# One row moved from TensorE to ScalarE and GpSimd, and a planned four-layer kernel put in a new order

## The chip, the core and the metric

The kernel runs on one core of a Trainium2 chip. Its engines work side by side, each through its own queue of instructions in order: TensorE (PE, with weight loads shown as PEld) multiplies matrices into PSUM, VectorE (DVE), ScalarE (ACT) and GpSimd (POOL) work element by element, and SyncE (SP) issues the transfers. They wait for each other by semaphores. The metric is the device time of one execution in microseconds, as the median of several runs; less is better.

## The reference

The input x has 128 graphs of 64 nodes with 512 features, in float32, and adj holds one 64 x 64 matrix for each graph. Four layers follow each other; each normalizes x, applies a ReLU, and adds its own result to x:

```python
# layer 0: H = (adj != 0); hconv(x, W) = D^-1 H B^-1 H^T (x W^T) + b
h = relu(layernorm(x)); t = layer_norm(relu(hconv(h, W1, b1)), gamma, beta)   # 512 -> 1024
x = x + hconv(t, W2, b2) + h                                                  # 1024 -> 512
# layer 1: s = (h w) a; A = softmax-like(tanh(s_i + s_j)) * adj
h = relu(layernorm(x)); x = x + A @ h @ w
# layer 2: attention with queries, keys and values, weight = adj * exp(q k)
h = relu(layernorm(x)); x = x + normalize(adj * exp((h Wq)(h Wk)^T)) @ (h Wv + bv)
# layer 3: transition P from adj * exp(leaky_relu(..)); three hops
h = relu(layernorm(x)); x = x + relu(sum_k (P^k h) Wk[k] + bk[k])
```

In layer 0 the inner normalization has a scale gamma and an offset beta for each of its 1024 features. The kernel folds them into the second product: W2's rows are multiplied by gamma, and the row beta x W2 (512 numbers) is added as a bias. That row is what the change computes in another way.

## The kernel before

The 8192 rows of x are cut into 16 groups of four tiles of 128 rows (two graphs a tile). All groups pass through layers 0 and 1 first, their x is stored to a scratch in DRAM, and then all groups pass through layers 2 and 3. The large products use Strassen's scheme: two tiles and two halves of the features make a 2 x 2 block, and seven products stand in for eight (`strassen`, L664, its matmuls at L682; `chained` for layer 2, L921; `product` for layer 3, L1087, its matmuls at L1112). The combinations of weights that the scheme needs are made once, in `combine` (L385), by VectorE subtractions at L394 to L397, for W1, W2 and w.

The functions of the layers don't issue instructions. They record operations in a `Graph`: an engine, an estimated cost, what is read and written, and a priority. `Graph.run` (L83) then plans: it keeps a clock for each engine and takes the operation that can start first by the estimates, and among equals the one with the lowest priority value. That order is written out into each engine's queue, and nothing in it moves at run time. A priority is the sum of a running value (`step`, scaled by `STRETCH`, with the group's `PERIOD1` or `PERIOD2`) and a shift, which `part(name)` (L294) takes from the table `AT` (L282). Buffers come from pools of few slots (`Buf`); which slot an operation gets is part of the plan, too.

The estimates are written beside the operations. A transfer costs its size at 380 KB per us or 0.34 us of SP, and lands `lat` later (2.0 us, or `LAT` = 2.5 in layers 2 and 3). Where the plan expects TensorE to stand for over 1 us and a PSUM slot is free, `fill` (L1183) puts matmuls of a 128 x 128 matrix of ones, the fillers (L1187), into the gap:

```python
        for _ in range(int(gap * FILL / (0.224 if filled else 0.448))):
            nc.tensor.matmul(ps[:, :P], ones, ones, start=True, stop=True)
```

Each float32 matmul shows as two instructions, two passes, in the profile.

What the change touches: `setup_l0` (L432) makes the row beta x W2. It multiplies each of the eight chunks of W2 (128 rows, 512 columns) by a one-column matrix from beta on TensorE (L438), copies the sum out of PSUM on ScalarE (L440), scales W2 in place by gamma on ScalarE (L442), and spreads the row over all partitions with a matmul against ones (L443) and a copy (L444). The row is the bias of `emit_y` (L710 on GpSimd, L712 on VectorE).

At the start, layer 2's weight matrix is made as well: `setup_l2` loads Wq and Wk in four pairs of blocks (into the four slots of `tmp`), multiplies them (L468), and stores the result (L475). `load_group` (L340, L346) loads adj and x of a group, `load_w` (L312) the weights.

Layer 1's matrix of a group (tile `bd`, L864) needs a row of denominators from another partition layout: `across` (L714) writes it to DRAM (L720) and reads it back spread out (L724). `left_mul_T` (L583) multiplies it with the tiles. `transposed` (L588) turns a tile by a ScalarE copy (L592), a transposing transfer (L593) and a second copy (L594). Layer 2 makes its sums of transposed tiles at L907.

Layer 3's weights are factors of seven 256 x 256 combinations, made during layers 0 and 1 by `setup_w3`, stored in DRAM, and streamed in again for every group: 14 loads a group at L1104, 768 or 576 KB, into three slots `wf`.

Of the kernel before, what the change touches and what calls it, by code (L numbers as in the profile page):

```python
# [10 lines left out]
AF = mybir.ActivationFunctionType  # L11
# [8 lines left out]
KD = D // P  # L20
KH = DH // P
# [147 lines left out]
def tile_adj_preln_d4(  # L169
# [6 lines left out]
    nc = tc.nc  # L176
# [33 lines left out]
    def size(shape):  # L210
        n = 1
        for d in shape[1:]:
            n *= d
        return n

    for two in TWO:
        both = work.tile([P, max(sum(size(shape) * n for _, shape, n in tags) for tags in two)], F32,
                         name="_".join(tag for tags in two for tag, _, _ in tags))
        for tags in two:
            at = 0  # L220
            for tag, shape, n in tags:
                for i in range(n):
                    v = both[:, at:at + size(shape)]
                    at += size(shape)
                    if len(shape) == 3:
                        v = v.rearrange("p (a b) -> p a b", a=shape[1])
                    elif len(shape) == 4:
                        v = v.rearrange("p (a b c) -> p a b c", a=shape[1], b=shape[2])
# [6 lines left out]
    w2m, wm = Buf("w2m"), Buf("wm")  # L235

    def view(mem, at, k, n):
        return mem[:, at:at + k * n].rearrange("p (c o) -> p c o", c=k)
# [3 lines left out]
    w2_sb = view(slots["w2m"][0], 0, KH, D)  # L242
# [9 lines left out]
    def c_mm(n, count):  # L252
        return 2 * count * max(n * 2 / 2400 + 0.0025, 0.111)
# [3 lines left out]
    def c_v(n, from_psum=False):  # L257
        return n / 960 + 0.155 + 0.05 * from_psum

    def pe(cost, fn, r, w):  # L260
        return G.op("PE", cost, fn, r, w)
# [4 lines left out]
    def act(cost, fn, r, w):  # L266
        return G.op("ACT", cost, fn, r, w)

    def pool(cost, fn, r, w):
        return G.op("POOL", cost, fn, r, w)  # L270

    def dma(kb, fn, r, w, issue=0.34, lat=2.0):
        return G.op("SP", max(kb / 380.0, issue), fn, r, w, lat)

    def quad(b):
        return b.t.rearrange("p (c k) -> p c k", c=4)

    FILL, LAT = 0.75, 2.5


    STRETCH, PERIOD1, PERIOD2 = (1.9884, 2.1221, 50.9861, 3.7462), 79.959, 161.557
    AT = {  # L282
        "x0": -2165.99, "apart": 359.07, "w1": 560.57, "b1": -128.79, "w2": 2266.0, "w": 629.08, "c1": 83.74, "l0":
        -235.81, "c2": 158.31, "l1": 2264.36, "c": -2424.06, "g0": -2117.86, "g1": -2122.8, "g2": -1819.53, "g3":
        -591.79, "g": -1886.72, "bq": -99.87, "l3": -7.89, "wg": -1139.97, "wp": 573.47, "beg0": -142.55, "beg1":
        62.01, "end00": -13.21, "end01": -32.01, "end11": -18.15, "new2": -7.11, "new3": -54.85, "end2": -9.77,
        "end3": 676.8, "load1": 485.14, "load2": 547.59, "m": -43.8, "h0": -30.46, "p0": -0.2, "z0": -80.08, "q0":
        9.15, "y0": -548.45, "h1": -32.41, "p1": -27.07, "z1": -26.16, "q1": -1.17, "y1": 3.58, "s": -28.4, "t0":
        14.62, "e0": 9.6, "t1": 5.71, "e1": -125.7, "hT": 311.43, "sh": 220.57, "lq": 604.06, "pt": 684.45, "v":
        70.12, "pv": 723.21, "s3": 659.55, "tt": 692.85, "a0": 741.32, "b0": -508.03, "a1": 777.21, "ws": 323.28,  # L290
        "load3": 129.62, "bk": 350.9,
    }

    def part(name):  # L294
        G.shift = AT[name]
# [4 lines left out]
    ones = const.tile([P, P], F32, name="ones")  # L300
# [13 lines left out]
    def wkeys(name, c0, c1):  # L314
        return [(name, c // 2) for c in range(c0 - c0 % 2, c1, 2)]
# [6 lines left out]
    def load_cols(name, src, k):  # L322
        sb = const.tile([P, k], F32, name=name)
        dma(8, lambda: nc.sync.dma_start(sb, src), [], [name])
        return sb
# [27 lines left out]
    def x_mid(g, t):  # L353
        return xmid[g, t], [("xmid", g, t)] + ([("xo", g - 1, t)] if g else [])

    part("x0")
    bq_c = load_cols("bq_c", bq, KD)
    load_group(0, x_in, AT["apart"])
    part("w1")
    load_w("w1", w1_sb, W1T)  # L360
# [3 lines left out]
    gb2 = const.tile([P, 2, KH], F32, name="gb2")  # L364
# [20 lines left out]
    def combine(name, w_, x_, kc, n, eng, olds=()):  # L385


        k2 = [w_[:, :kc, :], w_[:, kc:, :]]
        blk = lambda i, j: k2[i][:, :, j * n:(j + 1) * n]
        sub = {"DVE": nc.vector.tensor_sub, "POOL": nc.gpsimd.tensor_sub}[eng]  # L390
        cost = c_v(kc * n) * (1 if eng == "DVE" else 2)
        low, high = wkeys(name, 0, kc), wkeys(name, kc, 2 * kc)
        T1 = (name, "T1")
        G.op(eng, cost, lambda: sub(x_[:, 1], blk(1, 1), blk(0, 1)), [*low, *high], [(name, "x1"), *olds])  # L394
        G.op(eng, cost, lambda: sub(blk(0, 1), blk(0, 1), blk(0, 0)), [*low, (name, "x1")], [T1, (name, "given")])
        G.op(eng, cost, lambda: sub(x_[:, 0], blk(1, 1), blk(0, 1)), [*high, T1], [(name, "x0")])
        G.op(eng, cost, lambda: sub(x_[:, 2], blk(1, 0), x_[:, 0]), [*high, (name, "x0")], [(name, "x2")])  # L397
        B = {"11": (lambda c: blk(0, 0)[:, c, :], low), "21": (lambda c: blk(1, 0)[:, c, :], high),
             "22": (lambda c: blk(1, 1)[:, c, :], high), "T1": (lambda c: blk(0, 1)[:, c, :], [T1])}
        for i, key in enumerate(("T2", "T3", "T4")):  # L400
            B[key] = (lambda c, i=i: x_[:, i, c, :]), [(name, f"x{i}")]
        return B
# [28 lines left out]

    def setup_l0():  # L432

        p, row, pb = Buf("ps"), Buf("o"), Buf("ps")

        def mm():
            for c in range(KH):
                nc.tensor.matmul(p.t[0:1, :], gb2[:, 1, c:c + 1], w2_sb[:, c, :], start=(c == 0), stop=(c == KH - 1))  # L438
        pe(c_mm(512, KH), mm, ["gb2b", *wkeys(w2m, 0, KH)], [p])
        act(0.6, lambda: nc.scalar.copy(row.t[0:1, :], p.t[0:1, :]), [p], [row])  # L440
        for c in range(KH):
            act(0.72, lambda c=c: nc.scalar.activation(w2_sb[:, c, :], w2_sb[:, c, :], AF.Copy, scale=gb2[:, 0, c:c + 1]), ["gb2g"], [(w2m, c // 2)])  # L442
        pe(c_mm(512, 1), lambda: nc.tensor.matmul(pb.t, ones[0:1, :], row.t[0:1, :], start=True, stop=True), [row], [pb])  # L443
        act(0.6, lambda: nc.scalar.copy(bw2_b.t, pb.t), [pb], [bw2_b])  # L444

    def spread(col, dst, r, key):
# [63 lines left out]
    fac = [[dram.tile([P, n * 3 * P], F32, name=f"fac{f}_{n}") for n in (4, 3)] for f in range(7)]  # L510
    BLOCKS, FACS = ((1, 2, 6, 5), (7, 3, 4)), ((0, 2), (0, 1))
# [58 lines left out]
    def pre_ln(g, t, stats=None):  # L570

        xx, h = xt[g, t], Buf("h")
        nm, rs = stats or pre_stats(g, t)
        act(0.82, lambda: nc.scalar.activation(h.t, xx.t, AF.Relu, bias=nm.t, scale=rs.t), [xx, nm, rs], [h])  # L574
        return h
# [424 lines left out]
    def layer3(g):  # L1000
# [5 lines left out]
        for t in range(T):  # L1006
            h = pre_ln(g, t, stats[t])
# [6 lines left out]
        dn, rn, tr, tt = Buf("col"), Buf("col"), Buf("bd"), Buf("tt")  # L1014
# [72 lines left out]
        def product(f, F, chain, first):  # L1087
            (A, B), (ka, kb) = F
            if first:
                banks[chain] = [Buf("ps"), Buf("ps")]  # L1090
            X = Buf("xi")
            lo, hi = (lambda f_: f_()[:, :, 0, :]), (lambda f_: f_()[:, :, 1, :])
            x2, x3, x4 = ((lambda i=i: X.t[:, i]) for i in range(3))
            sub = nc.vector.tensor_sub
            dve(0.6, lambda: sub(x2(), lo(B), lo(A)), [*ka, *kb], [(X, 0)])
            dve(0.6, lambda: sub(x3(), hi(B), x2()), [*kb, (X, 0)], [(X, 1)])
            dve(0.6, lambda: sub(x4(), hi(A), x2()), [*ka, (X, 0)], [(X, 2)])
            lhs = {1: (lambda: lo(A), ka), 2: (lambda: hi(A), ka), 6: (x2, [(X, 0)]), 5: (lambda: lo(B), kb),
                   7: (x3, [(X, 1)]), 3: (x4, [(X, 2)]), 4: (lambda: hi(B), kb)}
            for n in range(2):  # L1100
                w_, p, q = Buf("wf"), banks[chain][n], len(BLOCKS[n])
                shift = G.shift
                part("ws")
                dma(q * 210, lambda n=n, w_=w_, q=q: nc.sync.dma_start(  # L1104
                    w_.t[:, :q].rearrange("p r k c -> p (r k c)"), fac[f - 1][n]), [("fac", f - 1, n, k, d) for k in range(3) for d in FACS[n]], [w_], lat=LAT)
                G.shift = shift
                for r, b in enumerate(BLOCKS[n]):
                    at, kl = lhs[b]

                    def mm(at=at, r=r, p=p, w_=w_, q=q):  # L1110
                        for k in range(3):
                            nc.tensor.matmul(inner(p, q)[:, r, :], at()[:, k, :], w_.t[:, r, k, :], start=first and r == 0 and k == 0,  # L1112
                                             stop=k == 2, skip_group_check=True)
                    pe(c_mm(P, 3), mm, [*kl, w_] if first and r == 0 else [*kl, w_, p], [p])
                    step(c_mm(P, 3))
# [53 lines left out]
        s3 = snapshot("X")  # L1169
# [9 lines left out]
    def step(us):  # L1179

        G.prio += us * stretch[0]
# [56 lines left out]
    for k in range(1, 3):  # L1238
        b = Buf("h")
# [71 lines left out]
```

## Time and profile before

| what | us |
|---|---|
| median of 3 runs | 2352.32 (2350.69 to 2354.56) |
| the profiled execution's own time | 2347.34 |
| its span, first to last instruction | 2345.6 |
| TensorE busy | 2301.3, 98% |
| VectorE busy | 1936.0, 83% |
| ScalarE busy | 1386.6, 59% |
| GpSimd busy | 1201.9, 51% |
| DMA: mean rate over the span | 151 GB/s |
| TensorE's granted clock, mean | 0.998 of full |

In the groups of instructions, a row gives the line, the engine, the operation, the tiles (result and sources), the count, then the busy time and the mean duration of one in ns, and behind the bar the idle time of the engine just before and what ended it. The time line has the start, the duration, the same names and count, and in brackets the idle time before. Tiles that share memory have a joint name: `w2m_wm_a_wf` holds W2 and w at first, and layer 3's operands and factors later. Fillers count as busy. Matmuls overlap, so the sum of their durations is larger than their busy time.

### The profile page before, as it was taken

What the parts mean: (1) busy time and instruction counts of PE and PEld (TensorE: products, weight loads), DVE (VectorE), ACT (ScalarE), POOL (GpSimd) and SP (SyncE); (2) the same over time, 40 slices, a digit from 0 to 9 for tenths busy, and PEclk for the clock granted to TensorE, in tenths of its full rate; (3) what the DMA queues carried; (4) which work ended last, traced back from release to release, by engine and by line L of the source; (5) the groups of instructions that cost most, each with busy time, mean ns of one, the idle gap of its engine ahead of it and who ended that gap; (6) DMA issues with size and microseconds to landing.
All of it is one profiled execution on the core that took longest, in us unless ns stands there. A gap on an engine that the chain in (4) does not pass through costs nothing.

```text
span 2345.6 us, 39929 instructions
## 1 busy us (share of the span) xinstructions
PE 2301.3 (98%) x14342; PEld 1876.8 (80%) x14342; DVE 1936.0 (83%) x4004; ACT 1386.6 (59%) x1986; POOL 1201.9 (51%) x1764
## 2 busy tenths in 40 slices
PE   9999999999999999999999999999999999999998
PEld 4676667776777767777688989999999999999998
DVE  7977887878878777787867888888889888888886
ACT  4656565665656756557556656655565656556642
POOL 5435566556565455553433554455455545455533
PEclk9999999999999999999999999999999999999999
DMA  7333342432333432223334888787888888798767
GB/s 265 85 76 74 82 103 72 106 83 72 95 84 99 89 77 69 70 73 66 89 89 134 235 230 224 211 223 207 242 231 220 230 213 215 211 252 227 214 184 234
DMA packets 403478, 355.13 MB, mean 151 GB/s; under 512 B 290896, under 2 KB 321872, under 8 KB 403280
## 3 DMA queue, kind: packets, MB, share of 16 engines
q1 hardware_dynamic: 403280, 352.58, 56.2%
q8 instruction: 113, 1.85, 0.3%
q14 instruction: 85, 0.70, 0.1%
HBM read 241.05 MB, written 44.33 MB: 122 GB/s over the span
## 4 chain that ended last, share of the span: by engine, by line
PE 75%; DMA 9%; DVE 9%; ACT 3%; POOL 2%; issue 2%; SPq 0%; DVEq 0%; POOLq 0%; ACTq 0%
PE ps L682 35%; PE ps L921 13%; PE ps L1112 13%; PE ps L583 5%; DMA w2m_wm_a_wf<-fac 4%; PE ps L1058 2%; PE ps L990 2%; DVE o L382 2%; PE ps L835 2%; DMA x<-xm 2%; PE ps L952 1%; DVE st L553 1%; DMA wa_q<-o 1%; PE ps L468 1%; DMA rw<-row 1%
## 5 line engine op out<-in xcount | busy, mean ns | idle before, releaser
L574 ACT ACTIVATE h<-x,nm,rs 128x512 f32<-128x512 f32 x384 | 307.0, 814 | 260.7 <-POOL nm L561 234.8
L1112 PE MATMUL ps<-w2m_wm_a_wf 128*128 128x128 f32 x2304 | 300.0, 276 | 3.8 <-DMA w2m_wm_a_wf<-fac 3.1
L1112 PEld LDWEIGHTS ps<-w2m_wm_a_wf 128*128 128x128 f32 x2304 | 279.4, 192 | 9.0 <-issue 2.0
L555 POOL TENSOR_SCALAR rs<-mv 128x1 f32<-128x1 f32 x320 | 102.5, 320 | 349.0 <-DVE mv L554 329.6
L682 PE MATMUL ps<-w2m_wm_a_wf,s_s_zz 128*128 128x256 f32 x1152 | 279.8, 380 | 0.7 <-DVE s_s_zz L674 0.5
L1112 PE MATMUL ps<-w2m_wm_a_wf,tmp_mB_xi 128*128 128x128 f32 x2016 | 262.3, 275 | 3.3 <-ACT h L574 1.7
L682 PEld LDWEIGHTS ps<-w2m_wm_a_wf,s_s_zz 128*128 128x128 f32 x1152 | 216.4, 190 | 48.1 <-issue 18.7
L1112 PEld LDWEIGHTS ps<-w2m_wm_a_wf,tmp_mB_xi 128*128 128x128 f32 x2016 | 244.9, 192 | 6.1 <-ACT h L574 3.0
L682 PE MATMUL ps<-w2m_wm_a_wf,rT_vu_tt 128*128 128x256 f32 x1024 | 237.2, 379 | 3.7 <-ACT rT_vu_tt L594 3.6
L682 PE MATMUL ps<-wa_mem,mT_sx 128*128 128x512 f32 x512 | 236.6, 593 | 0.2 <-ACT mT_sx L585 0.2
L682 PEld LDWEIGHTS ps<-w2m_wm_a_wf,rT_vu_tt 128*128 128x128 f32 x1024 | 193.2, 190 | 44.6 <-issue 12.4
L556 POOL TENSOR_TENSOR rs<-rs,mhalf 128x1 f32<-128x1 f32 x320 | 213.5, 667 | 26.6
L553 DVE BATCH_NORM_STATS2 st<-x 128x6 f32<-128x512 f32 x256 | 173.2, 680 | 17.0 <-DMA x<-xm 11.2
L682 PE MATMUL ps<-wa_mem,s_s_zz 128*128 128x512 f32 x384 | 180.0, 597 | 0.5 <-DVE z_hT L702 0.4
L682 PEld LDWEIGHTS ps<-wa_mem,mT_sx 128*128 128x128 f32 x512 | 96.9, 190 | 102.0 <-issue 96.6
L561 POOL TENSOR_SCALAR nm<-mv,rs 128x1 f32<-128x1 f32 x320 | 160.9, 504 | 30.4
L710 POOL TENSOR_TENSOR u<-u,row_sh 128x256 f32<-128x256 f32 x96 | 77.7, 822 | 170.7 <-DVE u L652 142.3
L592 ACT COPY o<-h 128x1024 uint16<-128x1024 uint16 x128 | 133.4, 1043 | 48.0 <-DVE h L1049 25.2
L583 PEld LDWEIGHTS ps<-bd,h 128*128 128x128 f32 x1024 | 128.7, 194 | 35.0 <-issue 17.1
L973 POOL TENSOR_TENSOR u<-u,wp_bv_bk 128x512 f32<-128x512 f32 x48 | 63.9, 1332 | 181.0 <-ACT u L625 180.8
L594 ACT COPY rT_vu_tt<-z_hT 128x1024 uint16<-128x1024 uint16 x128 | 147.8, 1160 | 10.8 <-DMA z_hT<-tmp_mB_xi 9.7
L822 ACT ACTIVATE z_hT<-z_hT,nm,rs 128x512 f32<-128x512 f32 x128 | 103.8, 813 | 73.3 <-POOL nm L561 73.3
(195 smaller groups left out, 5085.5 us busy)
## 6 DMA issues: line engine op xcount, KB each, us to landing
w2m_wm_a_wf<-fac SPq DMA_DIRECT2D x112, 768.0 KB, 5.8
w2m_wm_a_wf<-fac SPq DMA_DIRECT2D x112, 576.0 KB, 5.0
x<-xm SPq DMA_DIRECT2D x128, 256.0 KB, 3.9
x<-in_x_dram SPq DMA_DIRECT2D x64, 256.0 KB, 2.8
xm<-x SPq DMA_DIRECT2D x64, 256.0 KB, 2.3
out_dram<-x SPq DMA_DIRECT2D x64, 256.0 KB, 4.1
adj<-in_adj_dram SPq DMA_DIRECT2D x32, 256.0 KB, 4.2
fac<-wp_bv_bk SPq DMA_DIRECT2D x63, 128.0 KB, 2.0
```

The lines of the kernel that those rows point to most:

```text
L553: dve(0.69, lambda i=i: nc.vector.bn_stats(st.t[:, i, :], src(i)), [r[i]], [(st, i)])
L555: pool(0.32, lambda: nc.gpsimd.tensor_scalar_add(rs.t, mv.t[:, 1:2], EPS), [mv], [rs])
L556: pool(0.65, lambda: nc.gpsimd.tensor_tensor(rs.t, rs.t, mhalf, ALU.pow), [rs], [rs])
L561: pool(0.47, lambda: nc.gpsimd.tensor_scalar(nm.t, mv.t[:, 0:1], rs.t, -1.0, op0=ALU.mult, op1=ALU.mult), [mv, rs], [nm])
L574: act(0.82, lambda: nc.scalar.activation(h.t, xx.t, AF.Relu, bias=nm.t, scale=rs.t), [xx, nm, rs], [h])
L583: nc.tensor.matmul(quad(p)[:, c, :], h.t[:, c * P:(c + 1) * P], rhs(), start=True, stop=True)
L592: act(1.05, lambda: nc.scalar.copy(u16(planes.t).rearrange("p (q c) -> p q c", q=2), u16(src()).rearrange("p (c q) -> p q c", q=2)), ksrc, ...
L594: act(1.16, lambda: nc.scalar.copy(u16(dst()).rearrange("p c (k q) -> p c k q", q=2), u16(back()).rearrange("p (q c r) -> p c r q", q=2, c ...
L682: nc.tensor.matmul(p.t[:, :n], lhs()[:, c, :], rhs(c), start=first and c == 0, stop=c == kc - 1, skip_group_check=True)
L822: act(0.72, lambda half=half, rs=rs, nm=nm: nc.scalar.activation(half(), half(), AF.Identity, bias=nm.t, scale=rs.t), [(z, j), rs, nm], [( ...
L921: nc.tensor.matmul(pair(p.t)[:, o, :], a, b, start=first and o == 0 and c == 0, stop=c == 1, skip_group_check=True)
L1112: nc.tensor.matmul(inner(p, q)[:, r, :], at()[:, k, :], w_.t[:, r, k, :], start=first and r == 0 and k == 0, stop=k == 2, skip_group_check ...
```

## The change

`setup_l0` makes the row beta x W2 by eight ScalarE copies of W2's chunks, each scaled by its column of beta, and seven GpSimd additions of these copies (128 x 512). The matmul that spreads the row now sums over all 128 partitions as well. Three estimates change: the fillers' share of a gap (`FILL`, 0.75 to 0.5), the landing time of the streamed factors (0.8 us later), and the cost of VectorE's weight combinations (1.25 times). The bias bq is loaded in another place of the plan. All priorities are new: `STRETCH`, the periods, and every entry of `AT` (some left out here). As the plan follows from these, the order of the instructions changes on every engine, and the number of fillers as well.

```diff
-    FILL, LAT = 0.75, 2.5
+    FILL, LAT = 0.5, 2.5
...
-    STRETCH, PERIOD1, PERIOD2 = (1.9884, 2.1221, 50.9861, 3.7462), 79.959, 161.557
+    STRETCH, PERIOD1, PERIOD2 = (2.2519, 8.2241, 53.4307, 3.8206), 87.555, 166.876
     AT = {
-        "x0": -2165.99, "apart": 359.07, "w1": 560.57, "b1": -128.79, "w2": 2266.0, "w": 629.08, "c1": 83.74, "l0":
+        "x0": -2117.99, "apart": 200.73, "w1": 455.23, "b1": 843.47, "w2": 3279.78, "w": 178.43, "c1": -941.54,
...
+    part("bq")
+    bq_c = load_cols("bq_c", bq, KD)
     part("x0")
-    bq_c = load_cols("bq_c", bq, KD)
     load_group(0, x_in, AT["apart"])
...
-        cost = c_v(kc * n) * (1 if eng == "DVE" else 2)
+        cost = c_v(kc * n) * (1.25 if eng == "DVE" else 2)
...
-        p, row, pb = Buf("ps"), Buf("o"), Buf("ps")
-
-        def mm():
-            for c in range(KH):
-                nc.tensor.matmul(p.t[0:1, :], gb2[:, 1, c:c + 1], w2_sb[:, c, :], start=(c == 0), stop=(c == KH - 1))
-        pe(c_mm(512, KH), mm, ["gb2b", *wkeys(w2m, 0, KH)], [p])
-        act(0.6, lambda: nc.scalar.copy(row.t[0:1, :], p.t[0:1, :]), [p], [row])
+        row, pb = Buf("o"), Buf("ps")
+        for c in range(KH):
+            b = Buf("h") if c else row
+            act(0.65, lambda c=c, b=b: nc.scalar.activation(b.t, w2_sb[:, c, :], AF.Copy, scale=gb2[:, 1, c:c + 1]), ["gb2b", (w2m, c // 2)], [b])
+            if c:
+                pool(1.35, lambda b=b: nc.gpsimd.tensor_add(row.t, row.t, b.t), [b, row], [row])
         for c in range(KH):
             act(0.72, lambda c=c: nc.scalar.activation(w2_sb[:, c, :], w2_sb[:, c, :], AF.Copy, scale=gb2[:, 0, c:c + 1]), ["gb2g"], [(w2m, c // 2)])
-        pe(c_mm(512, 1), lambda: nc.tensor.matmul(pb.t, ones[0:1, :], row.t[0:1, :], start=True, stop=True), [row], [pb])
+        pe(c_mm(512, 1), lambda: nc.tensor.matmul(pb.t, ones, row.t, start=True, stop=True), [row], [pb])
...
-                    w_.t[:, :q].rearrange("p r k c -> p (r k c)"), fac[f - 1][n]), ..., [w_], lat=LAT)
+                    w_.t[:, :q].rearrange("p r k c -> p (r k c)"), fac[f - 1][n]), ..., [w_], lat=LAT + 0.8)
```

## The prediction

> **What bounds the kernel now.** I read the page's busy table first, then one line per stage, then TensorE's waits, and then the time line at the places that the change touches. Lines are those of the kernel before, unless said.
>
> ```profile
> PE 2301.3 (98%) x14342; PEld 1876.8 (80%) x14342; DVE 1936.0 (83%) x4004; ACT 1386.6 (59%) x1986; POOL 1201.9 (51%) x1764
> ...
> 0.00:180.00 180.00, 169.62 (x684) 110.07 (x685) 143.75 (x300) 98.99 (x139) 85.07 (x131) 0.98 0.48 141
> 180.00:1120.00 940.00, 936.53 (x4069) 672.79 (x4068) 755.68 (x1638) 577.54 (x806) 522.31 (x799) 1.00 0.35 82
> 1120.00:1330.00 210.00, 203.91 (x1263) 171.85 (x1262) 162.69 (x336) 127.01 (x180) 86.65 (x144) 1.00 0.49 132
> 1330.00:2260.00 930.00, 915.85 (x7625) 849.31 (x7624) 808.94 (x1611) 557.41 (x820) 476.98 (x652) 1.00 0.80 219
> 2260.00:2345.00 85.00, 75.38 (x707) 72.80 (x706) 64.95 (x123) 25.62 (x41) 30.91 (x42) 0.99 0.77 239
> ```
>
> TensorE bounds every stage (columns: window, its length, busy time of PE, weight loads, DVE, ACT, POOL; then granted clock, DMA share, GB/s). It idles 10.4 us in the first 180 us, 3.5 in the steady part of layers 0 and 1, 6.1 at the passage to layers 2 and 3, 14.1 in their steady part, 9.6 at the end: 44 us in all. That, the work taken off PE and the fillers are all that can be won.
>
> ```profile
> L1187 PE MATMUL ps<-ones 128*128 128x128 f32 x226 | 29.3, 287 | 1.0 <-DVE ones L301 1.0
> L438 PE MATMUL ps<-w2m_wm_a_wf,gb 128*1 128x512 f32 x16 | 7.0, 592 | 0.0
> ...
> PE ps L1112 <- DMA w2m_wm_a_wf<-fac: 9.6, 17, 1.3
> PE ps L583 <- DVE bd L864: 6.6, 7, 2.1
> PE ps L682 <- ACT rT_vu_tt L594: 3.6, 2, 2.6
> ```
>
> The fillers are 113 matmuls (two passes each), the one-column row eight. The three largest waits are for the streamed factors (17 times), for the matrix of layer 1, and for a transposed copy.
>
> ```profile
> 7.93 8.80 PE L468 MATMUL ps<-tmp_mB_xi 128*128 128x512 f32 x16 [2.95 <-DMA tmp_mB_xi<-in_Wk_dram]
> ...
> 43.60 7.03 PE L438 MATMUL ps<-w2m_wm_a_wf,gb 128*1 128x512 f32 x16
> ...
> 67.59 1.99 PE L682 MATMUL ps<-w2m_wm_a_wf,rT_vu_tt 128*128 128x256 f32 x8 [2.61 <-ACT rT_vu_tt L594]
> ...
> 151.44 5.40 PE L583 MATMUL ps<-bd,h 128*128 128x128 f32 x32 [2.08 <-DVE bd L864]
> ...
> 1246.89 5.52 PE L1187 MATMUL ps<-ones 128*128 128x128 f32 x48
> 1252.25 3.65 PE L921 MATMUL ps<-z_hT,wa_mem 128*128 128x256 f32 x16
> ```
>
> The row's matmuls have PE to themselves: nothing hides them. Some fillers end in a wait (67.59, 151.44), so they stood in time that was lost anyway; at 1246.89 the next matmul follows at once, so there the fillers may have held ready work.
>
> **Part by part.** I compare the two written orders. "Distance" is PE work between two instructions, a pass taken at 0.429 us for 512 columns, 0.216 for 256 and 0.111 for 128 (spacing of starts in the time line). By it PE has 2292.1 us of work before and 2272.3 after: 6.9 less for the row, 12.9 less for 58 fillers (113 become 55). Nothing else is taken off PE.
>
> (1) The row: 16 passes at 0.429 go, -6.9. The last matmul (L443) has 128 rows now instead of one, and the same 512 columns: 0.
>
> (2) What the row costs elsewhere. ACT gets eight copies; their nearest row is the scaling L442, 0.706 us each: 5.6 us. The scaling of a chunk, and DVE's combinations of W2, now wait for them; but the chunks land at 37 to 44 us, and ACT is busy 21.6 of the 40 us from 20 to 60. POOL gets seven additions of 128x512 like L799 (1.27 us; 1.47 in the first 180 us): 8.9 to 10.3 us. Five of them stand behind eight L799 and two groups of statistics, and the first L799 waited for its row until 45.1: 13 additions and 2.7 us of statistics end between 64 and 67. L443, behind which all of PE's queue stands, is reached after 36.3 us of PE work from the first product of layer 0, which I put at 25.0 in (3): at 61.3. So PE waits 3 to 5.5 us there. At the same place of the old order it waits 2.6 + 0.7 us (67.59, and the matmul after it), with 0.9 us of fillers ahead. One wait replaces the other: net 0, bounds -4 to +3.
> DVE meets the additions too: a combination (L395) took 2.27 us beside a POOL addition, and its neighbour 1.23 without: 1.04 each, 7.3 for seven. DVE is busy 37.8 of the 40 us from 20 to 60, so part of it reaches PE: +2, bounds 0 to +7.
> The Trainium skill ("SBUF — State Buffer", "Who interferes with whom") says that a VectorE instruction with two SBUF inputs and a GpSimd instruction that reads SBUF exclude each other for a whole instruction. By that rule the term would have 8.9 us of DVE time instead of 7.3, on the side against the change; the row says that less than a whole addition was lost. With the same part of it reaching PE the sum would be -12.6 by the rule and -13.0 by the row.
>
> (3) The start. Wq and Wk now lead SP's queue, ahead of adj and bq. The first 256 KB landed 3.2 us after its issue (1.18 to 4.40), the next 0.7 later, so L468 can start at 4.7 instead of 7.93. W1 goes behind the second weights, w and the second group: SP reaches it near 14.7 instead of 7.8, its halves land near 21.5 and 24.2 (18.4 before), and three combinations at the 5.7 us they took give T2 at 29.9. PE wants T2 at 30.2: just covered, and without that cover each us later is a us lost. So layer 0's first product moves from 28.5 to 25.0: -3.5, bounds -3.6 to 0.
>
> (4) The fillers. At the 13 places, the time from the first filler to the next real matmul sums to 38.6 us; without the first place (6.9, in (3)) and the one at 63.8 (3.8, in (2)) it is 27.9 us for 100 fillers, 0.28 each. The code sets fillers by the expected wait times FILL, so at 0.5 one filler stands for 1.5 times as much, 0.42. After has 46 beside the two places: 19.3 us. -8.6. Bounds: 0, if every filler dropped turns into idle; -12.0, if all 54 had held ready work.
>
> (5) The streamed factors. Their buffers are three; a load can start when the last matmul on its buffer is done. The distance from there to the first use is under 5.5 us (5.8 and 5.0 us from issue to landing) for 45 of 221 loads before, and for 18 after; those 18 are all near the end, as before. The steady part lost 7.3 us in 12 of the 17 waits: -5.5, bounds -7.3 to 0. The end keeps its 2.3 us.
>
> (6) Handoffs that are tighter. In the steady part of layers 0 and 1, the matrix of layer 1 (L864) is done 1.18 us ahead of its matmul (L583) by the order before, 0.20 after, in each of 11 groups. At 1.18, four groups waited 1.7 us in sum, since the two DMAs ahead of L864 vary (5.7 to 7.0 us from L862 to L864). +6, bounds 0 to 11. In layers 2 and 3, the last transposed copy (L594) stands 0.28 us ahead of L921 instead of 0.71 in 13 groups: +2.5, bounds 0 to 5.6. The sums L907, 0.63 instead of 2.28 ahead, waited already (2.8 us in 7): +1, bounds 0 to 8.
>
> (7) The clock: after the 2.1 us wait at 151.44, 32 passes took 5.40 us, and 3.73 at 71.24. Fewer fillers may add one such loss, or the shorter wait may drop it: 0, bounds -1.7 to +3.4.
>
> SP and POOL otherwise issue the same loads, stores and transposes in another sequence; between factor loads they stand much as before, so 0.
>
> Sum: -6.9 + 0 + 2 - 3.5 - 8.6 - 5.5 + 9.5 + 0 = -13.0. The profiled execution (span 2345.6, own time 2347.34) would come to 2334. It is 5 us under the median of the runs, 2352.32, and below all three; against that median I forecast 2339.
>
> **Rivals.**
> The fillers stood in real waits, and the start's gain is eaten by the late W1. Then (3) and (4) are 0 and -0.9 is left: 2351. For it: four of the places end in 1 us or more of idle. Against it: 47 of the fillers are followed at once by real work.
>
> Slower, by one mechanism: the transposed copy of layer 2. L594 waits for a DMA transpose, which SP issues in order behind factor loads that wait for PE (258.6 us of SP's waits). If the copy is 2 us late in each of 13 groups, PE stands 26 us: 2352.3 - 15.5 + 26 = 2363. It decides from 1.6 us a group on. For it: the distance was cut to 0.28. Against it: 0.71 gave one wait of 0.02 us in all of the steady part.
>
> The sums come later than I have them and L443 holds PE's queue: 10 us more than in (2) give 2349, 15 us 2354. For it: POOL's order has eight additions of b2 ahead of five sums. Against it: POOL was busy 25.9 of the 40 us from 20 to 60.
>
> **How the numbers follow.** A measurement here tells 0.2% (4.7 us) from no change. My forecast 0.58, with its own range 2322 to 2347; the fillers' rival 0.20, spread over faster, same and slower by 0.06, 0.09, 0.05; the copy 0.15, slower; the late sums 0.07, at 0.02, 0.02, 0.03. Faster 0.66, same 0.11, slower 0.23. All bounds together give -35 and +31; that all fall to one side is not to be expected, and 2320 to 2364 leaves out 2 in 10: the worse half of the copy's case and the late sums, and the better end of my own.
>
> **What would show it.** (1) no matmul of one column, eight ACT copies of 0.7 us. (2) L443 near 61 to 67 us, with a wait on POOL. (3) first L468 near 4.7, first product of layer 0 near 25. (4) fewer fillers and no longer idle after them. (5) waits for the factors at 2 to 4 us, at the end only. (6) waits of L583 for L864 in most groups, 0.3 to 1 us. (7) a clock at 1.0 beyond the first 20 us. I am wrong if the steady stages together idle over 30 us (17.6 now), or if the first product of layer 0 isn't earlier than 28.

## The result, and the profile after

The changed kernel takes 2364.26 us (median of 5 runs, 2358.70 to 2364.82), the kernel before 2352.72 on the same chip. The ratio is 1.0042, with a 95% interval of 1.0028 to 1.0057: slower by some 10 us, where I had forecast 13 us less. The profiled execution of the changed kernel is one of median time (span 2362.4); that of the kernel before lies 5 us under its median, so the two spans differ by 16.8.

The page's busy table, and the same stages as before (columns: window, its length, busy time of PE, weight loads, DVE, ACT, POOL; then granted clock, DMA share, GB/s):

```profile
PE 2289.1 (97%) x14210; PEld 1863.7 (79%) x14210; DVE 1938.5 (82%) x4004; ACT 1392.7 (59%) x1993; POOL 1212.5 (51%) x1771
```

```profile
0.00:180.00 180.00, 163.45 (x640) 105.92 (x641) 151.52 (x304) 104.22 (x147) 99.78 (x140) 0.98 0.48 141
180.00:1120.00 940.00, 934.83 (x4067) 672.49 (x4066) 774.63 (x1642) 581.68 (x804) 535.93 (x804) 1.00 0.34 82
1120.00:1330.00 210.00, 202.25 (x1214) 169.16 (x1213) 157.47 (x341) 131.36 (x187) 76.33 (x137) 0.98 0.51 133
1330.00:2260.00 930.00, 901.66 (x7493) 833.69 (x7492) 776.70 (x1572) 543.29 (x805) 461.79 (x643) 1.00 0.78 219
2260.00:2362.00 102.00, 86.87 (x802) 82.48 (x800) 78.14 (x149) 32.16 (x51) 38.65 (x49) 1.00 0.65 200
```

TensorE works 12.2 us less (2301.3 to 2289.1), and idles 29.3 us more: by stages 16.6, 5.2, 7.8, 28.3 and 15.1 us, against 10.4, 3.5, 6.1, 14.1 and 9.6. Half of it is new in the steady part of layers 2 and 3. The starts of the first sum L907 of a group say the same: between the fourth and the fifteenth group, 11 groups take 758.3 us before (1394.06 to 2152.37), 68.94 each, and 774.3 after (1392.25 to 2166.51), 70.39 each. At the fourth group the changed kernel is ahead by 1.8 us; over the 11 groups it loses 16.0, and behind them 2.7. This one execution shows less of a lead than the order has: at the third group it is 5.0 us ahead (1317.38 against 1322.35), while three of the later runs whose order is the same up to there (`copy_first`, `sums_first`, `both_first`: 1309.33, 1309.07, 1313.19) are ahead by 9.2 to 13.3. So the changed kernel comes to layers 2 and 3 with a lead, and loses more than that in them.

TensorE's waits over the whole run (total, times, longest):

```profile
PE ps L921 <- DVE row_sh L907: 22.0, 13, 2.3
PE ps L1037 <- DVE rT_vu_tt L1027: 8.4, 13, 2.6
PE ps L1112 <- DMA w2m_wm_a_wf<-fac: 8.3, 10, 3.1
PE ps L682 <- DVE u L654: 5.9, 4, 3.6
PE ps L583 <- DVE bd L864: 4.8, 7, 1.3
```

The sums L907 of layer 2 have taken the first place, with one wait in nearly every group (3.2 us in 8 waits before); the second, L1037 for L1027, stood at 0.2. I look at one steady group. VectorE's time line in it (start, duration, line, operation, tiles):

```profile
1526.96 1.67 DVE L383 SCALAR_TENSOR_TENSOR o<-h,c_b 128x512 f32<-128x512 f32 x1
...
1528.56 0.93 DVE L1049 TENSOR_TENSOR h<-h 128x256 f32<-128x256 f32 x1
1529.41 0.68 DVE L1131 TENSOR_TENSOR s_s_zz<-ps,s_s_zz 128x512 f32<-128x512 f32 x1
1530.01 0.89 DVE L1047 TENSOR_TENSOR h<-h 128x256 f32<-128x256 f32 x1
1530.82 1.21 DVE L383 SCALAR_TENSOR_TENSOR o<-h,c_b 128x512 f32<-128x512 f32 x1
...
1531.97 0.68 DVE L975 TENSOR_TENSOR rT_vu_tt<-ps,u 128x512 f32<-128x512 f32 x1
1532.57 0.68 DVE L907 TENSOR_TENSOR row_sh<-z_hT 128x512 f32<-128x512 f32 x1
```

ScalarE's and TensorE's in the same group:

```profile
1529.52 1.05 ACT L592 COPY o<-h 128x1024 uint16<-128x1024 uint16 x1 [1.65 <-DVE h L1049]
1530.47 1.16 ACT L594 COPY z_hT<-h 128x1024 uint16<-128x1024 uint16 x1
...
1533.30 1.99 PE L921 MATMUL ps<-wa_mem,row_sh 128*128 128x256 f32 x8 [2.06 <-DVE row_sh L907]
```

TensorE wants the first sum at 1531.24 and gets it at 1533.25. VectorE has no gap ahead of it: the dot products L383, which take 0.68 us alone, take 1.67 and 1.21, and L1049, L1047, L383 and L975 stand ahead of the sums. In all 12 steady groups these durations are the same within 0.02 us. In the kernel before only one dot product stands directly ahead of the sums, stretched as well (1462.02, 1.12 us); L1049 (1470.83), L1047 (1473.44) and L975 (1476.43) follow them, and the matmul that needs the sums starts without a wait. Its VectorE and TensorE at that place:

```profile
1462.02 1.12 DVE L382 SCALAR_TENSOR_TENSOR o<-h,c_b 128x512 f32<-128x512 f32 x1
1463.07 0.68 DVE L907 TENSOR_TENSOR row_sh<-z_hT 128x512 f32<-128x512 f32 x1
...
1464.53 3.72 PE L921 MATMUL ps<-row_sh,wa_mem 128*128 128x256 f32 x16
```

In the changed kernel the copy that the sums read (L594) is late too, by way of another engine: it stands on ScalarE behind L592, which waits for VectorE's L1049.

### The profile page after: what moved, and what is told of

The parts are those of the page before. It is cut to its first block, busy times and chain, and to the rows that moved or that the text cites. A ratio compares the mean times of both kernels' runs of the same rounds, so it can differ in the third digit from the quotient of the medians.

```text
span 2362.4 us, 39758 instructions
## 1 busy us (share of the span) xinstructions
PE 2289.1 (97%) x14210; PEld 1863.7 (79%) x14210; DVE 1938.5 (82%) x4004; ACT 1392.7 (59%) x1993; POOL 1212.5 (51%) x1771
## 3 DMA queue, kind: packets, MB, share of 16 engines
q8 instruction: 112, 1.84, 0.3%
## 4 chain that ended last, share of the span: by engine, by line
PE 67%; DVE 16%; DMA 9%; issue 3%; ACT 3%; POOL 2%; SPq 0%; DVEq 0%; ACTq 0%; POOLq 0%
PE ps L682 32%; PE ps L1112 13%; PE ps L921 11%; PE ps L583 4%; PE ps L1058 2%; DVE o L383 2%; DMA w2m_wm_a_wf<-fac 2%; PE ps L990 2%; PE ps L835 2%; DMA rw<-row 2%; DVE st L553 2%; DVE rT_vu_tt L1027 1%; DMA wa_q<-o 1%; DMA row<-col 1%; DVE tmp_mB_xi L1097 1%
## 5 line engine op out<-in xcount | busy, mean ns | idle before, releaser
L574 ACT ACTIVATE h<-x,nm,rs 128x512 f32<-128x512 f32 x384 | 302.2, 812 | 133.4 <-POOL nm L561 111.2
L682 PE MATMUL ps<-w2m_wm_a_wf,s_s_zz 128*128 128x256 f32 x1152 | 277.4, 380 | 0.2
L682 PEld LDWEIGHTS ps<-w2m_wm_a_wf,s_s_zz 128*128 128x128 f32 x1152 | 217.1, 190 | 44.1 <-issue 13.3
L682 PE MATMUL ps<-wa_mem,mT_sx 128*128 128x512 f32 x512 | 242.3, 597 | 7.7 <-DVE u L654 5.3
L682 PE MATMUL ps<-w2m_wm_a_wf,rT_vu_tt 128*128 128x256 f32 x1024 | 243.4, 382 | 0.9 <-DVE u L654 0.6
L682 PEld LDWEIGHTS ps<-w2m_wm_a_wf,rT_vu_tt 128*128 128x128 f32 x1024 | 193.8, 191 | 57.7 <-issue 30.7
L553 DVE BATCH_NORM_STATS2 st<-x 128x6 f32<-128x512 f32 x256 | 174.4, 685 | 17.5 <-DMA x<-xm 11.9
L682 PEld LDWEIGHTS ps<-wa_mem,mT_sx 128*128 128x128 f32 x512 | 96.3, 191 | 107.7 <-issue 88.0
L682 PE MATMUL ps<-wa_mem,s_s_zz 128*128 128x512 f32 x384 | 178.6, 593 | 2.4 <-DVE s_s_zz L674 2.4
L809 ACT ACTIVATE z_hT<-z_hT 128x512 f32<-128x512 f32 x128 | 80.1, 629 | 164.5 <-DVE z_hT L702 163.5
L561 POOL TENSOR_SCALAR nm<-mv,rs 128x1 f32<-128x1 f32 x320 | 151.0, 472 | 31.3
L592 ACT COPY o<-h 128x1024 uint16<-128x1024 uint16 x128 | 133.6, 1044 | 39.4 <-DVE h L1049 30.1
L594 ACT COPY rT_vu_tt<-z_hT 128x1024 uint16<-128x1024 uint16 x128 | 145.9, 1164 | 18.4 <-DMA z_hT<-tmp_mB_xi 17.9
L710 POOL TENSOR_TENSOR u<-u,row_sh 128x256 f32<-128x256 f32 x96 | 87.5, 926 | 123.6 <-DVE u L652 98.1
L921 PE MATMUL ps<-wa_mem,row_sh 128*128 128x256 f32 x512 | 121.0, 385 | 22.2 <-DVE row_sh L907 22.0
```

Of the source, the lines that this page charges most:

```text
L553: dve(0.69, lambda i=i: nc.vector.bn_stats(st.t[:, i, :], src(i)), [r[i]], [(st, i)])
L561: pool(0.47, lambda: nc.gpsimd.tensor_scalar(nm.t, mv.t[:, 0:1], rs.t, -1.0, op0=ALU.mult, op1=ALU.mult), [mv, rs], [nm])
L592: act(1.05, lambda: nc.scalar.copy(u16(planes.t).rearrange("p (q c) -> p q c", q=2), u16(src()).rearrange("p (c q) -> p q c", q=2)), ksrc, ...
L594: act(1.16, lambda: nc.scalar.copy(u16(dst()).rearrange("p c (k q) -> p c k q", q=2), u16(back()).rearrange("p (q c r) -> p c r q", q=2, c ...
L682: nc.tensor.matmul(p.t[:, :n], lhs()[:, c, :], rhs(c), start=first and c == 0, stop=c == kc - 1, skip_group_check=True)
L710: pool(0.75, lambda: nc.gpsimd.tensor_add(U.t[:, iv], U.t[:, iu], row()[:, cols]), [u, krow], [v])
```

## The experiments

All are edits of one of the two kernels. Ratios are to the kernel before, run on the same chip; the changed kernel's is 1.0042 [1.0028, 1.0057]. "Group" is the time of one of the 11 groups named above. In kernels with added lines the numbers of lines are larger by up to 12; the text names them by the lines of the changed kernel.

**The copy and the sums earlier in their queues.** A helper moves an instruction up past `hop` others of its engine, after the planning; all else keeps the changed kernel's order.

```diff
+        for x in [x for x in order if x[2].hop]:
+            i, n = order.index(x), x[2].hop
+            j = i
+            while n:
+                j -= 1
+                n -= order[j][2].eng == x[2].eng
+            order.insert(j, order.pop(i))
...
+            G.ops[-1].hop = 1 if t == T - 1 and 3 <= g < NG - 1 else 0      # copy_first: the last L594 of hT
...
+            G.ops[-1].hop = 2 if 3 <= g < NG - 1 else 0                     # sums_first: L907
```

> In 12 steady groups of layers 2 and 3 the last copy of hT (L594) goes one place up in ScalarE's queue, ahead of the split copy L592 that waits there 1.65 us for VectorE's L1049; all else keeps the changed kernel's order. Theory 'two queues' (PE's new wait of 19.9 us at L921 is made by VectorE's queue and by ScalarE's queue together): alone it brings nothing, 0 to -3 us, because the sums L907 still stand behind L383 and L975 on VectorE, which end at 1532.57 in the group that I looked at. Rival 'the copy alone' (the copy is what the sums wait for): the wait falls by about 1 us a group, -12. Rival 'not there' (the loss is not in this wait): 0.

> In the same 12 groups the four sums L907 go two places up in VectorE's queue, ahead of L383 and L975; the copy L594 stays behind L592. Theory 'two queues': the first sum can start when the copy ends (1531.63 instead of 1532.57 in that group), so about 0.9 us a group are won, -8 to -11. Rival 'VectorE's queue alone': the whole wait goes, -18 to -20. Rival 'not there', or 'the delay moves on' (L383, L975 and what follows them now come 2.8 us later and PE waits for those): 0 or slower.

> Both moves together. Theory 'two queues': the first sum ends at about 1531.5 where PE wants it at 1531.24, so 1.5 to 1.75 us in each of 12 groups are won: -18 to -21, the kernel near 2344 and below the kernel before by 6 to 9. The wait of L921 for L907 falls from 22 to under 5. Rival 'the delay moves on': the wait reappears at L990 (for L975) or L1058, and less than 8 us are won.

Measured: the copy alone 1.0038 [1.0026, 1.0051], the sums alone 1.0057 [1.0042, 1.0072], both 1.0045 [1.0029, 1.0060]; groups of 70.81, 70.87 and 70.80. Nothing is won, where the theory of two queues wanted nothing from the copy alone, but 8 to 11 us from the sums and 18 to 21 from both. TensorE's waits in the steady part, with the sums moved alone (its L929 is L921, its L630 ScalarE's copy of u, L623, and its L914 the sums):

```profile
PE ps L929 <- ACT u L630: 14.4, 12, 1.2
PE ps L929 <- DVE row_sh L914: 5.9, 7, 1.6
```

The wait for the sums fell from 19.9 to 5.9 us, and 14.4 us of waits for ScalarE have come in its place, once a group. The delay moves on, as the rival had it, but by way of ScalarE, which the rival didn't name. The link shows in ScalarE's queue: L592 waits for L383, though it needs nothing from it. Both write into slots of `o`, L383 the products that nobody reads. So a later L383 holds ScalarE's queue. From 1330 to 2250 us these waits sum to 6.0 us in the changed kernel, 18.4 with the copy moved, 40.2 with the sums moved and 48.5 with both. One of them, with the sums moved (its L599 is L592, its L390 L383):

```profile
1528.65 1.04 ACT L599 COPY o<-h 128x1024 uint16<-128x1024 uint16 x1 [3.35 <-DVE o L390]
```

**The additions thinned, on both kernels.** The edit leaves most of GpSimd's additions L1140 to L1143 and L973 out in the steady groups (each of the two places has its own K).

```diff
-            z = lambda a, b, s=1: Z.t[:, a:b:s]
+            z = lambda a, b, s=1: Z.t[:, a:b:s, :K]
+            K = 8 if 2 <= g < NG - 1 else P
...
+        K = 16 if 3 <= g < NG - 1 else D // 2
...
-                pool(1.42, lambda: nc.gpsimd.tensor_add(pair(U.t[:, iv]), pair(U.t[:, iu]), bias()), [u, bv_b], [v])
+                pool(1.42, lambda: nc.gpsimd.tensor_add(pair(U.t[:, iv])[:, :, :K], pair(U.t[:, iu])[:, :, :K], bias()[:, :, :K]), [u, bv_b], [v])
```

> The order of the changed kernel, but GpSimd's additions of the output (L1140 to L1143) and of layer 2's values (L973) handle an eighth or less of their columns in the steady groups, so most of this work is left out. Theory 'stretched by additions' (VectorE is late at L907 because L383, L1049 and L1047 take 1.67, 0.93 and 0.89 us beside GpSimd's additions instead of 0.68 and 0.5): VectorE reaches L907 1.5 to 2 us earlier, the wait shrinks from 19.9 to under 8, -10 to -16 us. Rival 'too much in the queue anyway': VectorE is as late as before, the wait stays above 15, and the time moves by less than 4.

> The kernel before, with the same of GpSimd's additions thinned as in the run 'thin' (most of L1140 to L1143 and L973 left out in the steady groups). There the changed kernel won some 33 us and its steady group of layers 2 and 3 went from 70.4 to 67.9 us; the group of the kernel before takes 68.8. Theory 'order times additions' (without the additions beside VectorE the two orders are equally good, TensorE bounds both): the group comes to 67.6 to 68.2, the time falls by 10 to 16 us. Rival 'the additions cost both the same': the group falls by 2.5 to 66.3, the time by 30 or more.

Measured: the changed kernel comes to 0.9905 [0.9884, 0.9926], 32 us less, where I had expected 10 to 16; the kernel before to 0.9968 [0.9952, 0.9983], 7.5 us less. The groups come to 67.87 and 68.48. In the steady part of the thinned changed kernel one wait for the sums is left, and the dot products have their short duration again (groups of instructions from 1330 to 2250 us, the dot products of the kernel before, where they are L382, of the changed kernel, and of the thinned changed one: count, busy time, mean ns of one; then TensorE's wait):

```profile
L382 DVE SCALAR_TENSOR_TENSOR o<-h,c_b 128x512 f32<-128x512 f32 x107 | 94.6, 902 | 0.9 <-DMA h<-o 0.9
```

```profile
L383 DVE SCALAR_TENSOR_TENSOR o<-h,c_b 128x512 f32<-128x512 f32 x104 | 94.5, 909 | 1.0 <-DMA wa_q<-o 0.9
```

```profile
L383 DVE SCALAR_TENSOR_TENSOR o<-h,c_b 128x512 f32<-128x512 f32 x109 | 74.8, 688 | 6.6 <-DMA wa_q<-o 5.7 <-DMA h<-o 0.4 <-ACT h L574 0.3
```

```profile
PE ps L921 <- DVE row_sh L907: 0.9, 1, 0.9
```

TensorE's waits for L1027, 5.8 us in the steady part of the changed kernel, are gone too, which the expectation had left out. So the order costs nothing by itself: without the additions the new one is the better by 0.6 us a group. The additions cost it 2.5 us a group and the old one 0.5 (7.5 us in all, where I had expected 10 to 16). The dot products are stretched alike in both, 902 and 909 ns on average; in the new order the stretch falls where TensorE waits for what comes next. The edit shortens GpSimd's own work as well, and doesn't separate that from the stretch: VectorE's waits for GpSimd's L1143 fell from 8.9 to 1.0 us. TensorE itself has no wait for GpSimd in its list.

**Undoing the link.** The dot products get a tile of their own for what nobody reads; the last kernel also moves the second half of L1027 ahead of two products (L960).

```diff
+    junk = const.tile([P, D], mybir.dt.bfloat16, name="junk")
...
-        dve(0.77, lambda: nc.vector.scalar_tensor_tensor(j.t, in0(), 1.0, in1(), op0=ALU.mult, op1=ALU.mult,
+        dve(0.77, lambda: nc.vector.scalar_tensor_tensor(junk, in0(), 1.0, in1(), op0=ALU.mult, op1=ALU.mult,
...
+            G.ops[-1].hop = 2 if i and 2 <= g < NG - 1 else 0               # all_first: L1027
```

> The changed kernel in its order; the dot products L383 write the products that nobody reads into a tile of their own (bf16) instead of a slot of o, which they share with ScalarE's split copies L592. So L592 no longer waits for a late L383 (0.5 us in the group that I looked at). Theory 'the queues are coupled through o': the copies come a little earlier, but the sums L907 still stand behind L383 and L975: 0 to -5. Rival 'o is the cause of the whole wait': -15 or more.

> As 'both_first' (the copy L594 one place up, the sums L907 two), with the tile of its own for the dot products. In 'both_first' the wait of 18 us at L921 for the sums became one of 14.2 us in 12 groups for ScalarE's copy of u, since L592 waited for the L383 that had been moved back, and ScalarE's queue with it. Theory 'the delay moved on through o': this wait falls under 4 us, the group from 70.7 to 69.4 to 69.8, the time by 10 to 14 against the changed kernel, to 0 to -4 against the kernel before. Rival 'VectorE has too much ahead of PE in any order of these few': another wait of 10 us or more takes its place, and the time stays.

> As 'both_junk', and the second half of L1027's transposes goes ahead of the two products L960 on VectorE, in groups 2 to 14, since TensorE waits 0.45 us for it in each group (5.4 to 6.8 us in all runs of the changed kernel). Theory: 3 to 5 us less than both_junk. Rival 'the delay moves on' to L990, which needs the products L960: 0.

Measured: the tile alone 1.0044 [1.0029, 1.0059]; with the copy and the sums moved 1.0007 [0.9997, 1.0016]; with L1027 as well 0.9988 [0.9978, 0.9998]. Groups of 70.48, 69.56 and 69.19. TensorE's largest waits in the steady part of the last (its L932 is L921, L632 is L623, L1001 is L990, L986 is L975):

```profile
PE ps L932 <- ACT u L632: 2.7, 9, 0.4
PE ps L1001 <- DVE rT_vu_tt L986: 2.7, 12, 0.2
```

That settles the chain. Neither the places in the queues nor the shared slots are enough alone, and together they give back 8 of the 10 us, where I had expected 10 to 14, and 13 with L1027; the last kernel is 0.12% faster than the kernel before (0.02 to 0.22%). That the new tile has another type (bf16) isn't what helps: with the tile alone the dot products still take 904 ns on average, and L592 waits for none of them. The delay has moved on a little even here, to L990 with 0.2 us a group, as the rival had it.

**The row.** Its copies and additions are left out, but for the first copy.

```diff
-            act(0.65, lambda c=c, b=b: nc.scalar.activation(
+            act(0.65, lambda c=c, b=b: c or nc.scalar.activation(
...
-                pool(1.35, lambda b=b: nc.gpsimd.tensor_add(row.t, row.t, b.t), [b, row], [row])
+                pool(1.35, lambda: None, [b, row], [row])
```

> The changed kernel in its own order, with seven of the eight copies L438 and all seven additions L440 left out, so the row is not the whole sum. Theory 'the additions slow VectorE at the start' (five of them run from 67.06 to 74.48 us, and beside them VectorE's L769 and L770 take 1.3 us each and TensorE waits 3.58 us for L654): the waits between 60 and 80 us fall by 3 to 5 us, and the time by 4 to 7. Rival 'VectorE is full there anyway': 0 to -2.

Measured: 1.0037 [1.0025, 1.0048], 1 us less than the changed kernel, which the intervals don't tell from nothing. The place is as expected, the total isn't. VectorE with the additions L440 (GpSimd's line first, then VectorE's), and without them:

```profile
67.06 7.42 POOL L440 TENSOR_TENSOR o<-o,h 128x512 f32<-128x512 f32 x5
...
67.57 2.69 DVE L769 TENSOR_SCALAR bd<-adj 64x256 f32<-64x256 f32 x2
70.28 1.32 DVE L770 TENSOR_SCALAR tmp_mB_xi<-adj 128x256 f32<-128x256 f32 x1
71.53 0.68 DVE L654 TENSOR_TENSOR u<-ps,u 128x512 f32<-128x512 f32 x1
```

```profile
67.71 0.58 DVE L769 TENSOR_SCALAR bd<-adj 64x256 f32<-64x256 f32 x2
68.30 0.29 DVE L770 TENSOR_SCALAR tmp_mB_xi<-adj 128x256 f32<-128x256 f32 x1
68.51 0.68 DVE L654 TENSOR_TENSOR u<-ps,u 128x512 f32<-128x512 f32 x1
```

L654 comes 3.0 us earlier, and TensorE idles 14.5 us in the first 180 instead of 16.6.

**The fillers**, in the changed kernel's order.

```diff
-    FILL, LAT = 0.5, 2.5
+    FILL, LAT = 0.75, 2.5
```

> The changed kernel with FILL at 0.75 again; the order is the same, 85 fillers instead of 55. Theory 'fillers stand in time that is lost' : 0 plus or minus 2 in sum, with the first 16 passes of L468 at 8.8 to 9.5 us instead of 10.06 (8.80 with 18 filler passes before them, 10.06 with 10), so -0.5 to -1.2 there. Rival, as my forecast had it: 0.28 us for each of 30 fillers, +8.

Measured: 1.0036 [1.0022, 1.0049], where the changed kernel has 1.0042. Thirty fillers more cost nothing, and save nothing that can be told. The 16 passes of L468 took 9.94 us, not the 8.8 to 9.5 that I had expected.

**The first transfers.** The pair of loads that the first pass of L468 needs goes to the front of SP's queue.

```diff
+            G.ops[-2].hop = G.ops[-1].hop = 0 if o else 3        # in setup_l2, the loads of Wq and Wk
```

> The changed kernel in its order, but the loads of Wq and Wk that the first pass of L468 needs go three places up in SP's queue and are now the first two (in the changed kernel they are the fourth and fifth transfers, and the first two feed the second pass). Theory 'wrong pair' (my forecast let L468 start when the first two transfers land, and they are the other pair): the first pass starts at 4.2 to 4.5 us instead of 6.76, the second waits for the other pair until 5.7 to 6.1; all 16 passes end 0.5 to 1.5 us earlier, and the total moves by less than 2, since layer 0 waits for VectorE later on. Rival 'the start counts in full': -2.4.

Measured: 1.0041 [1.0027, 1.0055]. TensorE's time line (its L476 is L468, its L789 L781):

```profile
4.32 8.82 PE L476 MATMUL ps<-tmp_mB_xi 128*128 128x512 f32 x16 [0.78 <-DMA tmp_mB_xi<-in_Wk_dram]
...
19.46 0.69 PE L789 MATMUL ps<-tmp_mB_xi,bd 128*64 128x65 f32 x16 [2.58 <-DVE tmp_mB_xi L783]
```

It was the wrong pair, as supposed. The passes start 2.4 us earlier and end 3.7 earlier (13.1 instead of 16.8), and the total doesn't notice: the next waits take more than half of it (layer 0's first product starts at 27.05 instead of 28.58), and the rest doesn't show in the total.

**VectorE's queue at the start**, on top of the last kernel.

```diff
+    for k, n in (269, 4), (276, 2), (278, 3):       # L674, L652, L654 of the first 75 us
+        G.ops[k].hop = n
```

> As 'all_first', and in the first 75 us three kinds of VectorE's work that TensorE waits for go ahead of work that nobody waits for soon: L654 ahead of the three products from adj (L769 twice, L770; they took 2.69 and 1.32 us beside the row's additions, and TensorE waited 3.58 us), L652 ahead of one L674 and one L485 (1.52), the first L674 ahead of four instructions (1.79). Theory 'the start's gain went into VectorE's queue': the three waits fall from 6.9 us to under 2, and 3 to 6 us are won against 'all_first' (0.9988 of the kernel before), so 0.996 to 0.9975, or 2341 to 2345 where the kernel before takes 2350.6. Rival 'the delay moves on': the products from adj come late for L781 or L583, a wait of 3 us or more takes their place, and the time stays within 1.5 us of 'all_first'.

Measured: 0.9985 [0.9974, 0.9996], where the kernel without these moves has 0.9988. The three waits fall from 6.9 to 1.1 us, and TensorE's time line has new ones, of 3.26 us here and of 1.03 at 77.28 (its L499 is L490, its L691 L682):

```profile
66.94 1.87 PE L499 MATMUL ps<-ones,o 128*128 128x1 f32 x8 [3.26 <-ACT c_b L461]
68.67 3.76 PE L691 MATMUL ps<-wa_mem,mT_sx 128*128 128x512 f32 x4
```

The rival holds, though the new wait is for ScalarE's `c_b` (L461) and not for the products from adj that it named: VectorE has 19.9 us of work in the 20 us from 60 to 80, here and in the changed kernel, so there the order mostly chooses who waits.

## Why the prediction was wrong, step by step

**(1) The row off TensorE, -6.9: right as work, open as time.** The one-column passes are gone. But in the first 80 us TensorE's idle time rose from 8.3 to 15.0 us: there, what it no longer works it waits, much of it for VectorE, which is busy 19.9 of the 20 us from 60 to 80. By the third group of layers 2 and 3 the changed order is ahead all the same, by 5.0 to 13.3 us; how much of that is this term, and how much the other fillers and waits on the way, no run separates.

**(2) The row elsewhere, +2 (0 to +7): right in size; the wait at L443, 3 to 5.5 us: not there.** L443 came at 79.31 instead of 61, and nothing waited at it. The additions were late too (the last ended at 74.48, not at 64 to 67), but TensorE had already lost time ahead of it to three waits for VectorE (1.52, 3.58 and 1.79 us, for L652, L654 and L674), which the sum didn't have. Without the copies and additions TensorE idles 2.1 us less in the first 180.

**(3) The start, -3.5: failed.** I let L468 start when the first two transfers land. Its first pass needs the second pair of loads, in both kernels, so it started at 6.76 and not 4.7; and the first product of layer 0 came at 28.58, as before (28.54). With the pair put right the passes start at 4.32, the first product at 27.05, and the total still stays.

**(4) The fillers, -8.6 (-12 to 0): failed, at its upper bound.** The rival "the fillers stood in real waits" is what the run shows: 55 or 85 of them make no difference. The whole step, 113 against 55 in one order, wasn't run.

**(5) The factors, -5.5: right in the steady part, not at the end.** Their waits fell from 7.3 to 2.2 us in it. At the end I let 2.3 us stand; it became 6.1, with waits of 3.08 and 1.84.

**(6) Handoffs, +9.5: the step that failed and decided it; its weights were wrong.** L864, priced at +6, went from 6.6 to 4.8 us. L594, at +2.5, ends no wait of its own that counts. "The sums L907, 0.63 instead of 2.28 ahead, waited already: +1, bounds 0 to 8" measured 17.1 us in the steady part (2.8 to 19.9) and 18.8 in all; and L1027 to L1037, which I had not listed at all, 8.2. The distance was counted in TensorE's work and took VectorE to be on time. It isn't: ahead of the sums stand L1049, L1047 and L975, which the old order has behind them, and its instructions there are stretched by GpSimd's additions (1.67 us for 0.68), and 2.28 us were what the old order kept for that. A place 0.20 ahead of its use (L864) lost no more than at 1.18 (4.8 us in all, 6.6 before), one 0.63 ahead (L907) lost 1.7 us in each of 12 groups: the distance says how much lateness is covered, and the lateness has to be read from the producing engine's own queue.

**(7) The clock, 0 (-1.7 to +3.4): too low, at its upper bound or over it.** Beyond the first 20 us, the one loss of the kernel before (1.7 us, behind 151.44) is gone, and two have come. After the wait of 3.58 us at 72.26, the next four passes took 3.78 us and eight shorter ones 2.75, where 1.88 and 1.89 are usual: 2.8 us. After a wait of 2.62 us at 1275.65, 16 passes of L1037 and 32 of L1058 took 1.12 and 3.78 us, where 0.69 and 2.06 are usual: 2.2 us, or 3.0 with the six fillers behind them. With the 1.7 off, that is 3.3 to 4.1 more.

The rival with the late copy of layer 2 had the place, and by luck nearly the time (2363): one lost wait in each of 13 groups at L921. Its mechanism isn't what the runs show: the copy moved ahead by itself won nothing, and ScalarE's waits for the transposes ahead of these copies fell (15.0 to 11.7 us from 1330 to 2250). Both things that I had said would prove me wrong came: 33.5 us of idle time in the steady stages, and a first product not earlier than 28.

## What to carry to other kernels

When an order changes, the room ahead of a handoff must be compared with how late the producing engine runs at that very place, with the durations that the trace has there and not the usual ones; VectorE beside GpSimd's additions needs about two microseconds of room at this place, by the 2.06 us that TensorE waited. An instruction that is moved up pushes others back, and a scratch slot that two engines share carries that delay into a third queue: look for such slots before moving anything. And work taken off one engine may come back as waiting in a stage where another is full, as VectorE is here from 60 to 80 us.

## What the runs showed of the hardware

An instruction with one tensor input is stretched as well: L769 took 0.29 us alone, and 2.69 for two beside the additions. The normalization's statistics (L553, one input) took 0.68 us, thinned or not, at most 0.70 in either. The Trainium skill ("SBUF — State Buffer", "Who interferes with whom") names both: `tensor_scalar` may use VectorE's second pair of ports, which it shares with GpSimd, and other instructions with one SBUF input do not contend. The traces agree with it.

The first 16 passes of L468 took 10.06 us in the changed kernel, but 8.61 to 9.81 in nine runs that share its start up to there and its 10 filler passes, and 9.94 with 16. So the 1.3 us that separate the two profiles at this place (8.80 before) are within what executions of one start differ by, and say nothing of the change.

How long TensorE waited doesn't tell by itself whether its clock drops. After 2.08 us (151.44 in the kernel before) the granted clock fell, to a mean of 0.72 from 150 to 156, and so it did after 2.62 us in the changed kernel (0.72 from 1272 to 1284), and after 3.26 and 3.58 us. After 2.61 us (67.59 in the kernel before) and 3.08 us (2311.59 in the changed one) it stayed at 1.00. The same wait of 2.62 us, in the run with the copy, the sums and the tile, left it at 1.00 (its L1048 is L1037; 1.12 us for these passes in the changed kernel):

```profile
1273.24 0.69 PE L1048 MATMUL ps<-rT_vu_tt,bd 128*64 128x64 f32 x16 [2.62 <-DVE rT_vu_tt L1038]
```

The Trainium skill ("TensorE: Matmul & The Clock Gate", "HAM oscillation — how this bites in real kernels") draws the line for an idle gap at about 3.4 us; the rows here show losses well below it, and no one line.
